# Subtracting the softmax maxima with 32-row products, maxima of the own chunk by query tile, and new durations for the planner

## The chip, the cores and the metric

One core of one Trainium2 chip runs the kernel. The metric is the device time of one execution in microseconds (us). The engines work side by side, each with its own list of instructions in a fixed order: PE (matrix products; its weight loads are listed apart as PEld), DVE (vector work), ACT (activations and copies), POOL (vector work away from the accumulators), SP (it issues the DMAs) and the DMA queues. Products accumulate in eight banks of 128 partitions by 512 fp32 words, which DVE and ACT read. Engines wait for each other by semaphores; while the first instruction of an engine's list waits, what is behind it waits too.

## The reference

Two transformer layers over 2048 tokens of width 256, each an attention and a gated FFN with layer norms around them. Layer 0 projects queries and keys through a small width with rotary parts, layer 1 through one matrix. What the change touches is the causal attention, which is the same in both layers: 16 heads of width 16.

```python
scores = jnp.einsum('bhqd,bhkd->bhqk', q_full, k_full) * scale
causal = jnp.tril(jnp.ones((T, T), dtype=bool))
scores = jnp.where(causal[None, None], scores, -jnp.inf)
probs = jax.nn.softmax(scores, axis=-1)
y = jnp.einsum('bhqk,bhkd->bhqd', probs, v)
...
x = x + _layernorm(_L0_attn_ref(_layernorm(x, axis=-1), ...), axis=-1)
x = x + _layernorm(_L0_ffn_ref(_layernorm(x, axis=-1), ...), axis=-1)
x = x + _layernorm(_L1_attn_ref(_layernorm(x, axis=-1), ...), axis=-1)
x = x + _layernorm(_L1_ffn_ref(_layernorm(x, axis=-1), ...), axis=-1)
```

## The kernel before

**Tiling.** The 2048 tokens are cut into four chunks `c` of 512 (`CH`), each of four tiles of 128 (`P`, `TPC = 4`). The 16 heads are four groups `g` of four; a group is two pairs `i` of two heads `e`. A unit is one chunk of queries with one group of heads: 16 units a layer, 32 in all, in the order (0,0), (0,1), all of chunks 1, 2 and 3, then (0,2), (0,3). Numbers are split into a high and a low half, so one head's scores contract over 64 rows (four products of halves of 16 values). Two heads of a pair thus lie on the two halves of the 128-row array: head `e` on rows 64e to 64e+63.

**One unit** has two parts.

The *maxima* (`maxima`) give each query's largest score. Queries are on the partitions. For every earlier chunk `p`, every query tile `t` and every head, one product of 64 rows by 512 keys fills a bank (L675) and DVE reduces it to one column of `pm` (L701, `pm<-banks 128x1<-128x512`). The own chunk is cut differently: `diagonal` writes the causal mask of all four diagonal tiles with a product of a 128x128 identity and `mask_qk` (L688, bf16, full array) and accumulates the four diagonal tiles of 128 keys onto it, the two heads by turns (L693); `block("b")` takes the keys left of the diagonal for query tiles 3 and 1 (384 and 128), `block("c")` those of tile 2 (256). DVE reduces each bank by 128-key tiles: the diagonals into column 1 of `pm`, the others into `pml`. `close` merges `pml` into column 0 of `pm` (three small reductions, also L701), takes the largest over all columns, and writes its negative as a high and a low half into `mx`. Four transposes (L737) and a copy on ACT (L741) turn it into `mrow`: rows 64e + 2i and 64e + 2i + 1 hold the two halves for head (i, e).

The *weighted sum* (`weighted`) goes over the 128-key tiles `kt`, up to the diagonal. Here keys are on the partitions. For each pair, a two-bank tile gets first the negative maxima, spread over all keys by a product with the selector `sel` that contracts over 64 rows, of which two hold something (L761, the shift), and then the scores on top (L766); both heads of the pair side by side, one on each half of the array. ACT takes the exponential into `pt` (L771). On a diagonal tile POOL zeroes what is masked (L775). Then the four heads' products with V (L782, 128 rows by 32 columns, four side by side, two instructions each) accumulate into one bank `av`, which is copied (L790), transposed (L795) and divided on DVE. On the last unit of a chunk follow the output projection, the norm and the sum with x (`mixed`).

**The order** of every instruction on every engine is written by a planner. Each piece of work is an `Op` with an engine, an estimated duration, the buffers that it reads and writes, a rank (lower is wanted earlier) and, on PE, a mode (`"row"`, `"col"` or `"full"`) and lanes (halves of the array). `Plan.run` simulates: of all ops that can start, it finds the earliest, and among ops of the same engine that could start up to `NEAR` later takes the lowest rank. `SWITCH` is what it allows for a change of mode, `HOP` for a semaphore, `lag` for an op's latency. Work comes out in exactly that order. Eight banks are shared; at most two two-bank tiles (`s`) are in use at a time. The maxima of a unit are ranked about one unit ahead of its weighted sum, so in a steady stretch PE mixes shifts, scores and V products of one unit with maxima of the next.

The FFN (`ffn`) has its own plan: for each chunk gate and up products (L912), SiLU and multiplication, splitting into halves (L923, L924), and the down product (L879). Projections and output products run through `products` (L553).

Of the kernel before, what the change touches and what calls it, by code (L numbers as in the profile page):

```python
# [132 lines left out]
class Plan:  # L133
# [3 lines left out]
    HOP, NEAR, SWITCH = 0.06, 0.3, 0.25  # L137

    def __init__(self):
        self.ops = []  # L140

    def op(self, engine, us, fn, r=(), w=(), after=(), hold=(), rank=0.0, mode=None, lanes=(0, 1), lag=0.0):
# [6 lines left out]
        o = Op(engine, us, fn, bufs, list(dict.fromkeys(deps)), rank, mode, lanes, lag)  # L149
# [9 lines left out]
    def run(self):  # L159
# [9 lines left out]
        while ready:  # L169
            best = []  # L170
            for o in ready:
# [26 lines left out]
                if o.engine == "PE":  # L198
                    at = max([at] + [free.get(("PE", x), 0.0) for x in o.lanes])
                    if o.mode != mode:  # L200
                        at = max([at] + [free.get(("PE", x), 0.0) for x in (0, 1)]) + self.SWITCH
                else:
                    at = max(at, free.get(o.engine, 0.0))
# [3 lines left out]
            at, o = min((p for p in best if p[1].engine == first[1].engine and p[0] <= first[0] + self.NEAR),  # L207
                        key=lambda p: (p[1].rank, p[0]))
# [27 lines left out]
def kernel(ctx: ExitStack, tc: tile.TileContext, x_in, cols_in, rows_in, wd_in, wuq_in, rot_in,  # L236
# [145 lines left out]
    ident16 = const.tile([P, P], BF16, tag="ident16", name="ident16")  # L382
    mask_qk = const.tile([P, TPC, P], BF16, tag="mask", name="mask")

    def make_mask():
        make_identity(nc, ident16)
        nc.gpsimd.memset(mask_qk, 0.0)
        nc.gpsimd.affine_select(out=mask_qk, in_=mask_qk, compare_op=ALU.is_ge, fill=NEG, base=0,
                                pattern=[[0, TPC], [-1, P]], channel_multiplier=1)

    mask_b = setup("POOL", 1.8, make_mask)


    sel_f = const.tile([P, 2, P], F32, tag="sel_f", name="sel_f")
    sel = const.tile([P, 2, P], F32R, tag="sel", name="sel")

    def make_sel():
        nc.gpsimd.memset(sel_f, 0.0)
        for e in range(2):
            for i in range(2):  # L400
                at = sel_f[64 * e:64 * e + 64, i, :]
                for row_ in (2 * i, 2 * i + 1):
                    nc.gpsimd.affine_select(out=at, in_=at, compare_op=ALU.not_equal, fill=1.0, base=-row_,
                                            pattern=[[0, P]], channel_multiplier=1)
        nc.gpsimd.tensor_copy(sel, sel_f)
# [4 lines left out]
    pms = [const.tile([P, TPC, 2, 2, NCHUNK + 1], F32, tag=f"pm{i}", name=f"pm{i}") for i in range(2)]  # L410

    def make_mx():
        for i in range(2):
            nc.gpsimd.memset(pms[i], NEG)
        for i in range(2):
            nc.gpsimd.memset(mx[i], 0.0)

    mx_b = setup("POOL", 1.6, make_mx)
# [27 lines left out]
    def normalize(plan, dst, src, rs, nm, i, r, w, rank):  # L446
        plan.op("ACT", 0.45, lambda: nc.scalar.activation(dst(), src(), AF.Identity, bias=nm.t[:, i:i + 1],
# [17 lines left out]
    def flipped(plan, src, hold, name, rank):  # L465

        banks = []
        for cc in range(2):
# [6 lines left out]
            plan.op("PE", 0.5, flip, r=[src], w=[s], hold=hold, rank=rank, mode="full", lag=0.2)  # L475
# [3 lines left out]
    def transposed(plan, src, name, rank):  # L479
        dst = wide_buf(f"T_{name}")  # L480
        for cc, s in enumerate(flipped(plan, src, [dst], name, rank)):
            plan.op("ACT", 0.59, lambda cc=cc, s=s: nc.scalar.copy(as_halves(dst.t)[:, cc, :], s.t), r=[s], w=[dst], rank=rank)
# [12 lines left out]
    def stacked(plan, c, what, s, i, bias, hi, lo, rank):  # L495

        plan.op("ACT", 0.69, lambda: nc.scalar.activation(as_halves(hi.t)[:, i, :], s.t, AF.Identity, bias=bias[:, i:i + 1]),
# [51 lines left out]
    def products(plan, s, us, terms, r, hold, rank):  # L549
# [5 lines left out]
        plan.op("PE", us, go, r=r, w=[s], hold=hold, rank=rank, mode="full", lag=0.2)  # L555

    def proj0(plan, c, rank, *dst):
# [23 lines left out]
        for i, (n, a, b) in ((1, (P, DQR, DC)), (0, (DQR, 0, DQR))):  # L581
# [6 lines left out]
            plan.op("PE", 0.5, flip, r=[cd, normed[i]], w=[s], hold=[cT], rank=rank, mode="full", lag=0.2)  # L588
# [56 lines left out]
    def attention(layer, plan, wo, wob, bo, scale):  # L645
        L, KS, Vs, kb, vb = layer.L, layer.K, layer.V, layer.kb, layer.vb
        with tc.tile_pool(name=f"kv{L}", bufs=1) as kv, tc.tile_pool(name=f"at{L}", bufs=1) as at:
# [4 lines left out]
            for tag in ("Q", "y", "pml", "mrow", "pt", "o"):  # L652
                rings.pop(tag, None)
            rpm, rmx = Ring(2), Ring(2)

            def maxima(n, c, g, qb):

                pm, mx_ = Buf(lambda: pms[n % 2], rpm), Buf(lambda: mx[n % 2], rmx)
                pml = new(at, [P, 2, 2, 6], F32, "pml", f"pml{L}{n}", 2)
                full = 2 * (2 * TPC * c + 6)  # L660
# [6 lines left out]
                def block(name, i, e, terms, us, reduces, red_us, kc, dst):  # L667

                    s = bank(f"m{L}{n}{i}{name}{e}")
                    b = 64 * e  # L670
                    rk = rank()

                    def fill():
                        for t, k0, k1, to in terms:
                            nc.tensor.matmul(s.t[:, to:to + k1 - k0], qb.t[b:b + 64, i, t * P:(t + 1) * P],  # L675
                                             KS[kc][b:b + 64, 2 * g + i, k0:k1], start=True, stop=True)

                    plan.op("PE", us, fill, r=[qb, kb[kc][g]], w=[s], hold=[dst], rank=rk, mode="row", lanes=(e,), lag=0.2)
                    plan.op("DVE", red_us, lambda: reduces(s.t), r=[s], w=[dst], rank=rk)

                def diagonal(i):

                    ss = [bank(f"m{L}{n}{i}d{e}") for e in range(2)]
                    rk = rank()

                    def fill():
                        for e in range(2):
                            nc.tensor.matmul(ss[e].t, ident16, mask_qk.rearrange("p t k -> p (t k)"), start=True, stop=False)  # L688
                        for t in range(TPC):
                            for e in range(2):  # L690
                                b = 64 * e
                                at_ = slice(t * P, (t + 1) * P)
# [405 lines left out]
```

## Time and profile before

| | |
|---|---|
| median of 3 runs | 1487.26 us (1486.95 to 1487.43) |
| the profiled execution | 1490.08 us |
| span of its instructions | 1488.4 us |
| mean granted clock of PE | 0.935 |
| shift products (L761) | 1280 instructions, 296.3 us busy |
| score products (L766) | 1280 instructions, 257.8 us busy |
| V products (L782) | 2560 instructions, 303.5 us busy |
| products for the maxima (L675, L693, L688) | 1152, 512 and 128 instructions; 261.8, 46.9 and 42.1 us busy |
| exponentials (L771, ACT) | 640 instructions, 548.1 us busy |
| reductions for the maxima (L701, DVE, large ones) | 1152 instructions, 687.5 us busy |

Busy times are sums of instruction records. On PE a record includes the time that a product waits in the array's pipe, and products on different halves overlap, so a record is longer than the pace at which products follow each other; the pace is read from starts. A group's line names the line of the code, the engine, the operation, its output and inputs with shapes, how often it runs, its busy time and mean, and the idle time of its engine before it with what ended it. `64*128 64x512` reads: 64 rows by 128 columns of the array, 512 columns streamed.

### The profile page before, as it was taken

The numbers are of one execution on the slowest core, as the hardware profiler recorded it, in microseconds if no ns is written. First come the engines' busy times: TensorE is split into PE (matmuls) and PEld (weight loads), VectorE is DVE, ScalarE is ACT, GpSimd is POOL, SyncE is SP. The second block draws the span as 40 slices with busy tenths as digits, with TensorE's granted clock in tenths as the row PEclk, the third lists the DMA queues.
The fourth block names the chain that finished last, engine by engine and source line by source line (L and its number), as shares of the span: only waits on it lengthen the run. The fifth ranks groups of instructions, "written<-read, shape, count | busy, mean of one in ns | idle before, by whom it ended". The sixth has DMA issues, their size and how long they took to land.

```text
span 1488.4 us, 22354 instructions
## 1 busy us (share of the span) xinstructions
PE 1325.1 (89%) x8632; PEld 740.4 (50%) x8632; DVE 934.5 (63%) x1932; ACT 798.0 (54%) x1094; POOL 289.6 (19%) x468
## 2 busy tenths in 40 slices
PE   2578999999999999959996999999999999995996
PEld 1344544544454444437764555455444444443875
DVE  1267679678888772424444756886888787333442
ACT  1232664556556668545551345555655666764563
POOL 3010111110001000235631101110000100023564
PEclk9687999899999999969997799999999999997998
DMA  4432230032000000020045023005000000000000
GB/s 148 173 134 90 73 141 28 2 125 75 15 15 1 15 15 16 1 71 0 1 170 212 15 91 122 15 15 183 17 15 15 1 15 15 15 1 1 1 29 29
DMA packets 42618, 78.74 MB, mean 53 GB/s; under 512 B 3891, under 2 KB 8336, under 8 KB 42384
## 3 DMA queue, kind: packets, MB, share of 16 engines
q1 hardware_dynamic: 42080, 75.85, 14.6%
q8 instruction: 67, 1.10, 0.3%
q0 software_dynamic: 144, 1.16, 0.2%
q10 hardware_dynamic: 288, 0.31, 0.1%
q14 instruction: 39, 0.32, 0.1%
HBM read 41.66 MB, written 35.65 MB: 52 GB/s over the span
## 4 chain that ended last, share of the span: by engine, by line
PE 64%; DVE 18%; ACT 6%; DMA 4%; POOL 3%; issue 3%; SPq 1%; POOLq 0%; ACTq 0%; DVEq 0%
PE banks L782 13%; PE banks L761 11%; DVE pm L701 11%; PE banks L675 9%; PE banks L766 8%; PE banks L553 8%; PE banks L912 5%; ACT pt L771 3%; PE banks L693 2%; DVE pml L701 2%; PE banks L688 2%; PE banks L879 2%; DMA Q<-sc_q 2%; PE banks L473 2%; PE banks L795 1%
## 5 line engine op out<-in xcount | busy, mean ns | idle before, releaser
L771 ACT ACTIVATE pt<-banks 128x1024 f32<-128x1024 f32 (+3 forms) x640 | 548.1, 895 | 362.2 <-PE banks L766 332.6
L701 DVE TENSOR_REDUCE pm<-banks 128x1 f32<-128x512 f32 (+1 forms) x896 | 557.8, 682 | 144.0 <-PE banks L675 73.4
L782 PE MATMUL banks<-pt,V 128*32 128x512 f32 (+3 forms) x2560 | 303.5, 545 | 6.7 <-POOL pt L775 6.4
L761 PE MATMUL banks<-mrow,sel 64*128 64x512 f32 (+3 forms) x1280 | 296.3, 429 | 14.6 <-DVE pm L701 5.2
L675 PE MATMUL banks<-K,Q 64*128 64x512 f32 (+3 forms) x1152 | 261.8, 414 | 16.7 <-ACT pt L771 3.5
L775 POOL TENSOR_SCALAR_AFFINE_SELECT pt<-pt 128x256 f32<-128x256 f32 x256 | 104.4, 411 | 870.2 <-ACT pt L771 868.0
L766 PE MATMUL banks<-Q,K 64*128 64x512 f32 (+3 forms) x1280 | 257.8, 373 | 0.0
L761 PEld LDWEIGHTS banks<-mrow,sel 64*128 64x128 f32 x1280 | 139.7, 191 | 197.1 <-ACT pt L771 99.2
L675 PEld LDWEIGHTS banks<-K,Q 64*128 64x128 f32 x1152 | 138.3, 192 | 142.7 <-DVE pm L701 62.1
L701 DVE TENSOR_REDUCE pml<-banks 128x4 f32<-128x512 f32 (+1 forms) x256 | 129.7, 549 | 95.1 <-PE banks L675 94.7
L766 PEld LDWEIGHTS banks<-Q,K 64*128 64x128 f32 x1280 | 143.6, 193 | 7.1
L782 PEld LDWEIGHTS banks<-pt,V 128*32 128x32 f32 x2560 | 52.4, 109 | 101.9 <-issue 76.0
L924 POOL TENSOR_TENSOR fl<-fu,fh 128x512 fp32r<-128x512 f32 x64 | 81.9, 1292 | 79.5 <-ACT fh L923 79.5
L921 DVE SCALAR_TENSOR_TENSOR fu<-banks,cols,sl 128x512 f32<-128x512 f32 x64 | 46.9, 747 | 58.1 <-ACT sl L919 42.0
L693 PE MATMUL banks<-K,Q 64*128 64x128 f32 x512 | 46.9, 307 | 32.1 <-DMA Q<-sc_q 32.1
L912 PE MATMUL banks<-fx,wg 128*128 128x512 f32 x256 | 73.9, 409 | 1.7 <-ACT sl L919 0.9
L912 PE MATMUL banks<-fx,wu 128*128 128x512 f32 x256 | 70.0, 396 | 0.0
L693 PEld LDWEIGHTS banks<-K,Q 64*128 64x128 f32 x512 | 37.5, 207 | 62.6 <-issue 49.8
L923 ACT CAST fh<-fu 128x512 fp32r<-128x512 f32 x64 | 39.5, 620 | 38.4 <-DVE fu L921 38.2
L912 PEld LDWEIGHTS banks<-fx,wg 128*128 128x128 f32 x256 | 48.7, 194 | 14.4 <-DVE fx L866 2.1
L912 PEld LDWEIGHTS banks<-fx,wu 128*128 128x128 f32 x256 | 49.4, 193 | 10.5
L919 ACT ACTIVATE sl<-banks,cols 128x512 f32<-128x512 f32 x64 | 43.1, 687 | 15.2 <-PE banks L912 14.9
(127 smaller groups left out, 1104.5 us busy)
## 6 DMA issues: line engine op xcount, KB each, us to landing
K<-sc_k SPq DMA_DIRECT2D x32, 512.0 KB
Q<-sc_q SPq DMA_DIRECT2D x32, 512.0 KB
sc_k<-kh SPq DMA_DIRECT2D x32, 256.0 KB
sc_k<-kl SPq DMA_DIRECT2D x32, 256.0 KB
sc_q<-qh SPq DMA_DIRECT2D x32, 256.0 KB
sc_q<-ql SPq DMA_DIRECT2D x32, 256.0 KB
x<-in_x_dram SPq DMA_DIRECT2D x4, 512.0 KB
out_dram<-x SPq DMA_DIRECT2D x4, 512.0 KB
```

What stands on the lines that cost most here:

```text
L553: nc.tensor.matmul(s.t[:, at:at + n], a, b, start=start, stop=stop)
L675: nc.tensor.matmul(s.t[:, to:to + k1 - k0], qb.t[b:b + 64, i, t * P:(t + 1) * P], KS[kc][b:b + 64, 2 * g + i, k0:k1], start=True, stop=True)
L693: nc.tensor.matmul(ss[e].t[:, at_], qb.t[b:b + 64, i, at_], KS[c][b:b + 64, 2 * g + i, at_], start=False, stop=t == TPC - 1)
L701: nc.vector.tensor_reduce(dst, src, AX.X, ALU.max)
L761: nc.tensor.matmul(s.t[:, e, 0:nq], sel[b:b + 64, i, :], mrow.t[b:b + 64, off:CH], start=True, stop=False)
L766: nc.tensor.matmul(s.t[:, e, 0:nq], KS[kt // TPC][b:b + 64, 2 * g + i, k * P:(k + 1) * P], qb.t[b:b + 64, i, off:CH], start=False, stop=True)
L771: plan.op("ACT", 0.19 + nq / 620, lambda s=s, pt=pt, nq=nq: nc.scalar.activation(pt.t[:, :, 0:nq], s.t[:, :, 0:nq], AF.Exp, scale=scale), ...
L775: plan.op("POOL", 0.41, lambda pt=pt: nc.gpsimd.affine_select(out=pt.t[:, :, 0:P], in_=pt.t[:, :, 0:P], compare_op=ALU.is_ge, fill=0.0, ba ...
L782: nc.tensor.matmul(av.t[32 * j:32 * j + 32, off:CH], Vs[kt // TPC][:, kt % TPC, DV * h:DV * h + 32], pts[kt, j // 2].t[:, j % 2, 0:nq], st ...
L912: nc.tensor.matmul(s.t[:, i, :], w[:, cc, fc * P:(fc + 1) * P], xT[j].t[:, cc, :], start=n == 0, stop=n == 3)
L921: plan.op("DVE", 0.75, lambda s=s, sl=sl, fu=fu, fc=fc: nc.vector.scalar_tensor_tensor(fu.t, s.t[:, 1, :], col(su_at + fc), sl.t, ALU.mult ...
L924: plan.op("POOL", 1.3, lambda fu=fu, fh=fh, fl=fl: nc.gpsimd.tensor_tensor(fl.t, fu.t, fh.t.bitcast(F32), ALU.subtract), r=[fu, fh], w=[fl ...
```

## The change

**Shifts.** The maxima's layout changes: head `h = 2i + e` of a group has its own 32 rows of `mrow` (rows 32h and 32h + 1 hold the two halves), and `sel` is one 128x128 tile with two rows of ones in each 32. A shift contracts over 32 rows; the two heads of pair `i` take rows 64i to 64i + 63, one half of the array. In the plan the shift becomes an op of its own with `lanes=(i,)`, ahead of the score op, which keeps both halves. Both have the mode `"row"`.

**Own-chunk maxima.** `diagonal` and `pml` go. Three blocks per head, `a` (query tile 3, 512 keys), `b` (tile 2 with 384 and tile 0 with 128) and `c` (tile 1 with 256), each write the mask for their diagonal tiles with two 64-row products (`half16` holds an identity cut in two halves of 64 rows), add the diagonal products, and then write the rest of the tile's keys. Each reduction covers one query tile's keys and writes column 0 of `pm`. All own-chunk blocks of a unit come first, then the other chunks.

**The planner.** New allowances for switching by the mode switched to, 0.11 us for a weight load, a latency for every op of DVE, ACT and PE; ops within 0.12 us of the earliest are considered instead of 0.3, and starting later is charged 0.3 of rank a microsecond (both 0.1 in the FFN's plan). ACT's estimated durations are some 0.09 us shorter.

```diff
-    HOP, NEAR, SWITCH = 0.06, 0.3, 0.25
-
-    def __init__(self):
-        self.ops = []
+    HOP, LOAD, SWITCH = 0.06, 0.11, {"row": 0.14, "col": 0.21, "full": 0.18}
+    LAG = {"DVE": 0.08, "ACT": 0.1, "PE": 0.2}
+
+    def __init__(self, near=0.12, waiting=0.3):
+        self.ops, self.near, self.waiting = [], near, waiting
...
                 if o.engine == "PE":
-                    at = max([at] + [free.get(("PE", x), 0.0) for x in o.lanes])
-                    if o.mode != mode:
-                        at = max([at] + [free.get(("PE", x), 0.0) for x in (0, 1)]) + self.SWITCH
+                    lanes, more = (o.lanes, 0.0) if o.mode == mode else ((0, 1), self.SWITCH[o.mode])
+                    at = max([at + self.LOAD] + [free.get(("PE", x), 0.0) + more for x in lanes])
...
-            at, o = min((p for p in best if p[1].engine == first[1].engine and p[0] <= first[0] + self.NEAR),
-                        key=lambda p: (p[1].rank, p[0]))
+            at, o = min((p for p in best if p[1].engine == first[1].engine and p[0] <= first[0] + self.near),
+                        key=lambda p: (p[1].rank + self.waiting * (p[0] - first[0]), p[0]))
...
-    ident16 = const.tile([P, P], BF16, tag="ident16", name="ident16")
-    mask_qk = const.tile([P, TPC, P], BF16, tag="mask", name="mask")
+    half16 = const.tile([P, 2, P], BF16, tag="half16", name="half16")
+    mask_qk = const.tile([P, 2, 2, P], BF16, tag="mask", name="mask")
...
-                def diagonal(i):
...
-                        for e in range(2):
-                            nc.tensor.matmul(ss[e].t, ident16, mask_qk.rearrange("p t k -> p (t k)"), start=True, stop=False)
-                        for t in range(TPC):
-                            for e in range(2):
-                                b = 64 * e
-                                at_ = slice(t * P, (t + 1) * P)
-                                nc.tensor.matmul(ss[e].t[:, at_], qb.t[b:b + 64, i, at_], KS[c][b:b + 64, 2 * g + i, at_],
-                                                 start=False, stop=t == TPC - 1)
...
+                        def part(t, k0, to, width, start, stop):
+                            nc.tensor.matmul(s.t[:, to:to + width], qb.t[b, i, t * P:(t + 1) * P],
+                                             KS[kc][b, 2 * g + i, k0:k0 + width], start=start, stop=stop)
+
+                        if kc < c:
+                            for t, k0, k1, to in terms:
+                                part(t, k0, to, k1 - k0, True, True)
+                            return
+
+                        lo = terms[0][3] + terms[0][2] - terms[0][1] - P
+                        for x in range(2):
+                            nc.tensor.matmul(s.t[:, lo:lo + P * len(terms)].rearrange("p (d k) -> p d k", k=P), half16[b, x, :],
+                                             mask_qk[b, x, 0:len(terms), :], start=x == 0, stop=False)
+                        for j, (t, k0, k1, to) in enumerate(reversed(terms)):
+                            part(t, k1 - P, to + k1 - k0 - P, P, False, j == len(terms) - 1)
+                        part(t, k0, to, k1 - k0 - P, True, True)
...
+                    for e in range(2):
+                        block("a", i, e, [(3, 0, CH, 0)], 0.45, c, [(0.6, 3, 0, slice(0, CH))])
+                    for e in range(2):
+                        block("b", i, e, [(2, 0, 3 * P, 0), (0, 0, P, 3 * P)], 0.8, c,
+                              [(0.47, 2, 0, slice(0, 3 * P)), (0.2, 0, 0, slice(3 * P, CH))])
+                    for e in range(2):
+                        block("c", i, e, [(1, 0, 2 * P, 0)], 0.4, c, [(0.34, 1, 0, slice(0, 2 * P))])
...
-                    for t, a, b in ((1, 3, 4), (2, 4, 6), (3, 0, 3)):
-                        top(pm.t[:, t, :, :, 0], pml.t[:, :, :, a:b])
...
+                        def shift(s=s, i=i, off=off, nq=nq):
+                            for e in range(2):
+                                b = slice(64 * i + 32 * e, 64 * i + 32 * e + 32)
+                                nc.tensor.matmul(s.t[:, e, 0:nq], sel[b], mrow.t[b, off:CH], start=True, stop=False)
+
+
+                        plan.op("PE", max(0.19, nq / 2220), shift, r=[mrow, sel_b], w=[s], rank=rk, mode="row", lanes=(i,))
+
                         def score(s=s, kt=kt, i=i, off=off, nq=nq):
-                            for e in range(2):
-                                b = 64 * e
-                                nc.tensor.matmul(s.t[:, e, 0:nq], sel[b:b + 64, i, :], mrow.t[b:b + 64, off:CH],
-                                                 start=True, stop=False)
...
-                        plan.op("PE", 2 * max(0.19, nq / 2380), score, r=[qb, mrow, kb[kt // TPC][g], sel_b], w=[s], rank=rk,
-                                mode="row", lag=0.2)
-                        plan.op("ACT", 0.19 + nq / 620, lambda s=s, pt=pt, nq=nq: nc.scalar.activation(
+                        plan.op("PE", max(0.19, nq / 2220), score, r=[qb, kb[kt // TPC][g], s], w=[s], rank=rk,
+                                mode="row")
+                        plan.op("ACT", 0.1 + nq / 620, lambda s=s, pt=pt, nq=nq: nc.scalar.activation(
...
-            plan = Plan()
+            plan = Plan(0.1, 0.1)
```

In the changed kernel the same work has other line numbers: shifts L753, scores L762, maxima L679, masks L689, V products L778.

## The prediction

> **What bounds the kernel now.** I read the page first: busy shares, then the chain of work that ended last.
>
> ```profile
> PE 1325.1 (89%) x8632; PEld 740.4 (50%) x8632; DVE 934.5 (63%) x1932; ACT 798.0 (54%) x1094; POOL 289.6 (19%) x468
> PE 64%; DVE 18%; ACT 6%; DMA 4%; POOL 3%; issue 3%; SPq 1%; POOLq 0%; ACTq 0%; DVEq 0%
> ```
>
> PE carries the end, DVE is second. A share over the whole span mixes stages, so next come busy times in four stretches: attention of layer 0, FFN, attention of layer 1, FFN (columns: stretch, length, each engine's busy time and instructions, granted clock, DMA share, GB/s).
>
> ```profile
> 95.00:655.00 560.00, 525.59 (x3754) 268.92 (x3752) 394.63 (x805) 320.32 (x412) 74.07 (x160) 0.95 0.14 50
> 655.00:800.00 145.00, 126.54 (x530) 95.30 (x530) 65.95 (x145) 76.78 (x134) 65.37 (x60) 0.94 0.21 73
> 800.00:1345.00 545.00, 515.92 (x3680) 260.68 (x3682) 385.13 (x760) 309.06 (x388) 64.58 (x135) 0.95 0.13 45
> ```
>
> Attention is 1105 of 1488 us; what the change touches lies there. DMA moves little, ACT has a third free. Then the chain by line in a steady part of it (950 to 1250 us, clock 1.00):
>
> ```profile
> by line: PE banks L782 17.9%; DVE pm L701 17.1%; PE banks L761 16.1%; PE banks L675 14.4%; PE banks L766 10.2%; ACT pt L771 5.6%; PE banks L553 4.7%; issue 3.9%; PE banks L693 2.2%; PE banks L688 1.9%; DVE pml L701 1.8%; PE banks L795 1.2%;
> ```
>
> The PE lines add up to 69%, DVE to 19%. So of a microsecond of PE work added or removed I count 0.69 on the path. A busy PE record includes waiting in its pipe, so prices come from starts. PE in order of time:
>
> ```profile
> 1171.25 0.62 PE L675 MATMUL banks<-K,Q 64*128 64x512 f32 x4
> 1171.81 1.07 PE L782 MATMUL banks<-pt,V 128*32 128x512 f32 x8
> ...
> 1173.14 0.41 PE L766 MATMUL banks<-Q,K 64*128 64x512 f32 x2
> 1173.37 0.41 PE L761 MATMUL banks<-mrow,sel 64*128 64x512 f32 x2
> 1173.60 0.41 PE L766 MATMUL banks<-Q,K 64*128 64x512 f32 x2
> ...
> 1177.98 0.60 PE L688 MATMUL banks<-mask,ident 128*128 128x512 bf16 x2
> 1178.51 0.66 PE L693 MATMUL banks<-K,Q 64*128 64x128 f32 x8
> 1179.01 0.45 PE L761 MATMUL banks<-mrow,sel 64*128 64x512 f32 x2
> ```
>
> Two 64-row products on the two halves of the array, 512 columns each, start a new pair every 0.23 us (1173.14, 1173.37, 1173.60), weights included. Four L675 before L782 take 0.56, that is 2 x 0.23 and 0.10 more: the array changes from 64 rows by 128 columns to 128 rows by 32. Two L688 before L693 take 0.53, 0.07 more: there the row height alone changes, 128 to 64. So a change of array form costs 0.07 to 0.10; I use 0.09. The eight L693 (four pairs of 128 columns) take 0.50, 0.125 a pair, against 128/512 x 0.23 = 0.055 of streaming: with short products the weight load sets the pace, 0.07 over the stream.
>
> **The change, part by part.** What follows counts along the order in which each kernel issues to PE.
>
> *Shifts.* There are 320 key tiles, of mean width 435 columns (139264 columns in all), 0.85 of 512. Before, each has two shift pairs, each filling both halves: 640 x 0.85 x 0.23 = 125 us. After, a pair fills one half, and two pairs can run side by side. Only 101 key tiles have all four shifts next to each other; the other 219 have them as 438 separate pairs with 64-row products, V products or transposes between. If a 32-row product doesn't share the array with 64-row ones, this is (101 + 438) x 0.85 x 0.23 = 105: **-20 us**. If it does, at best 320 x 0.85 x 0.23 = 63: -62.
>
> *Changes of form.* If 32 rows and 64 rows are two forms, the order has 1488 changes after against 851 before (729 of the new ones between 32 and 64 rows): 637 x 0.09 = **+57 us**. If they are one form, 759: -92 x 0.09 = -8. No 32-row product is in this trace. The lower bound of a 32-64 change is 0 (L766 to L761 goes from one half's products to the next without a gap), the upper is 0.10 of L675 to L782; the nearest row is L688 to L693, row height alone, and it pays. So I take 0.09, and the other end is the first rival.
>
> The Trainium skill, TensorEngine Tiling (Array Packing), section Key Properties, says that changing the tiling mode, and not just the tile, drains the array, and its Available Configurations list 32x128 apart from 64x128. That agrees with the 0.07 to 0.10 and speaks against this change; without that rule the sum would be the rival's. TensorE: Matmul & The Clock Gate, Measured speedup vs the span model, gives 3.07 times for four 32-row products side by side, not 4; by it the 101 full runs would take 0.30 instead of 0.23 each, an estimate of 6 us more. No run here shows either for 32 rows.
>
> *Maxima over other chunks* (768 products of 512 columns). Their work is the same, but shifts now stand between the two halves' products: a run of them takes the fuller half, and these add up to 459 slots before, 558 after: 99 x 0.23 = **+23 us**. With one form the neighbour fills the half: 0.
>
> *Own-chunk maxima.* Per pair of heads, before: two 512-column masks, four 128-column pairs alternating between the halves, then 384, 128 on each half and 256 on each. PE starts in order, so a half's product runs beside the other's last one only: 1024 + 512 + 1152 = 2688 columns. After, each half gets its whole block (4, 5 or 4 products) before the other: counted the same way 3200 columns. 512 more columns are 0.23 us, x 64 pairs: +15. Loads: ten of the 26 products are 128-column f32r ones, 0.07 over stream each, against 4 x 0.07 before: 0.42 x 64 = +27. Bounds: 0 if the loads hide, +63 if the eight 128-column mask products pay too; I take the middle one, because the mask's weights are bf16 and their load record is half as long (L688 101 ns on average, L693 207). Together **+42 us**.
>
> Sum on PE: -20 + 57 + 23 + 42 = +102, x 0.69 = **+70 us**.
>
> *DVE.*
>
> ```profile
> L701 DVE TENSOR_REDUCE pm<-banks 128x1 f32<-128x512 f32 x768 | 476.8, 681 | 74.6 <-PE banks L675 73.4 <-PE banks L766 0.2
> L701 DVE TENSOR_REDUCE pml<-banks 128x4 f32<-128x512 f32 x128 | 82.5, 682 | 51.0 <-PE banks L675 50.8
> L701 DVE TENSOR_REDUCE pml<-banks 128x2 f32<-128x256 f32 x128 | 49.7, 416 | 44.2 <-PE banks L675 43.9
> L701 DVE TENSOR_REDUCE pm<-pml x96: 143/152/164, 88.1 to 1339.3; 128x4 f32<-128x4 f32 x32, 128x4 f32<-128x8 f32 x32, 128x4 f32<-128x12 f32 x32
> ```
>
> The 96 merges of pml go: -96 x 0.152 = -15 us. Per head the reduces were 512, 512, 256 wide (0.685 + 0.682 + 0.416 = 1.78 us) and become 512, 384, 128, 256: the 384 one lies between 0.416 and 0.681 (0.55), the 128 one between 0.152 and 0.416 (0.28), 1.93: +0.15 x 128 = +19. Net +4, x 0.19 = **+1**. The merges stood before the transpose of the maxima (L737), so that latency shortens by 0.45 us a unit, 32 units; PE has scores of the unit before to run there, so I count nothing (14 us if that cover were gone).
>
> *Nothing:* ACT keeps its 961 issues and SP its 171; the DMA order differs in five places, and DMA is 13% busy. The set-up on POOL (mask, selector, zeroing) is about the same few microseconds between 10 and 17 us, long before the first mask product at 58 us. The split of shift from score adds no semaphore wait: the wait for the bank pair (freed by the exponential, L771) and for mrow moves to the shift, the wait for Q and K to the score. What is queued behind either on PE is the next maxima or V product; DVE waits for the first, ACT for the second, which frees its output buffers.
>
> *The planner.* New durations, a narrower choice and a penalty for waiting change the order on all engines, FFN too. A better order can only take what PE waits for others: the shift's weight loads sat 104 us until the exponential and 62 until a maximum, 166 in all, but they are loads, and mostly hidden. I take a twentieth, **-8**, with bounds -40 (a quarter) and +20 (the new planner knows no 32-64 change, so its times are off by 0.09 at each of 729).
>
> Sum: 70 + 1 - 8 = +63. The profiled execution took 1490.1 (span 1488.4 and 1.7 around it), 2.8 over the median of the runs, 1487.3; the difference goes on the median: **1550 us**. With the bounds (changes at 0.07, loads 0, planner -40, and half of it on the path; or 0.10, 63, +20 and all on the path) this case runs from 1495 to 1610.
>
> **Rivals.** *32 and 64 rows share the array without a change (faster).* For: 64-row products of the two halves run side by side, and a shift sits in one half. Against: L688 to L693 pays for row height alone. Price on PE: between -62 + 42 - 8 = -28 and, counted along the order with both halves free (row-form products and masks take 406 us at 0.23 for 512 columns, before 434; loads +27, changes -8), -9; the middle -18 x 0.69 = -12, planner -8: **1467**, 1440 to 1490. It decides from a 32-64 change below about 0.01 us.
>
> *PE's waits swallow it.* DVE's 19% and ACT's 6% of the chain become the bound and PE's 102 us fall into its waiting. Against: PE lines are 69% of the chain. Then +1 - 8: 1480; with part of it, **1490**.
>
> *The weight load can't be fetched ahead over a 32-64 change.* Each would show a load record, 0.19 us (L761 PEld), instead of 0.09: 637 x 0.10 x 0.69 = 44 more, **1594**, up to 1640. For: loads are ahead only if their rows are free. Against: at L675 to L782 a load of 0.11 and a change fit in 0.10.
>
> **How the numbers follow.** Forecast 0.62; one form 0.28; swallowed 0.06; load exposed 0.04. About 0.2% (3 us) is what a measurement tells from no change. Faster: 0.25 of the second, 0.02 of the third and 0.01 of the first, 0.28; within 0.2%: 0.05; slower: 0.67. The range 1455 to 1605 leaves out about 0.07 below (the one-form case with a good plan) and 0.09 above. Both signs hold much of the chance; the likeliest case's own range is 1495 to 1610.
>
> **What would show it.** From the start of a shift pair (L753) to the following score (L762), without a wait between: 0.32 if it is a change of form, 0.23 if not. A 64-row product right behind a shift on the other half: starting with it, or 0.3 later. Own-chunk blocks: 2.1 us per pair of heads, or 1.4. PE's share of the chain should rise above 69% in the steady stretch. Wrong would be: shifts starting beside maxima of the other half; or PE no longer in the chain.

## The result, and the profile after

| | before | after |
|---|---|---|
| median of the runs taken together | 1487.11 us (1484.84 to 1487.43, 4 runs) | 1610.45 us (1593.79 to 1620.85, 4 runs) |
| ratio of the fast runs, 95% interval | 1 | 1.0796 (1.0703 to 1.0888) |
| the profiled execution, its span | 1490.08, 1488.4 | 1593.79, 1592.1 |
| mean granted clock of PE | 0.935 | 0.920 |

The change costs 8%. One run of after (1620.85 us) counts as slow, being over 1.5% above its quickest; the other three have a median of 1605.1 us (1593.79 to 1615.8), 118 us over before, and what follows goes by these. The profiled execution is the quickest of all, so its trace explains 104 us of the 118.

The page of after, busy shares and then the chain that ended last, by engine:

```profile
PE 1442.5 (91%) x9272; PEld 789.6 (50%) x9272; DVE 938.2 (59%) x1964; ACT 794.7 (50%) x1094; POOL 289.3 (18%) x468
PE 75%; DVE 8%; DMA 5%; ACT 4%; issue 3%; POOL 2%; SPq 2%; POOLq 0%; ACTq 0%; DVEq 0%
```

PE is 117 us busier, DVE and ACT within 4 us of what they were, and DVE's part of the chain went from 18% to 8%: PE has become the bound outright. By stage (stretch, length, each engine's busy time and instructions, granted clock, DMA share, GB/s; the same four stages as before, the last FFN left out):

```profile
95.00:700.00 605.00, 578.26 (x3989) 286.23 (x3987) 391.54 (x792) 318.25 (x410) 72.16 (x150) 0.93 0.13 46
700.00:850.00 150.00, 133.86 (x549) 99.83 (x550) 64.07 (x145) 77.24 (x135) 65.23 (x67) 0.92 0.21 71
850.00:1450.00 600.00, 575.52 (x4005) 285.59 (x4003) 390.15 (x788) 305.95 (x384) 62.92 (x136) 0.93 0.12 42
```

Attention went from 560 to 605 us in the first layer and from 545 to 600 in the second: 100 of the 104 us, with DVE's and ACT's work in it within some 5 us of what it was. The chain by line in a steady part of the second (1110 to 1240 us; clock 0.50 in its first 13 us, 1.00 behind):

```profile
by line: PE banks L778 25.4%; PE banks L679 22.4%; PE banks L753 19.3%; PE banks L762 12.6%; DVE pm L697 7.5%; PE banks L557 2.8%; PE banks L689 2.7%; ACT pt L767 2.7%; issue 1.7%; PE banks L791 1.5%; PE banks L729 1.4%; ACTq L767 0.0%; DVE
```

PE's lines add up to 88% (before: 69%). What PE holds up is the exponential. Its row in before and in after:

```profile
L771 ACT ACTIVATE pt<-banks 128x1024 f32<-128x1024 f32 (+3 forms) x640 | 548.1, 895 | 362.2 <-PE banks L766 332.6
L767 ACT ACTIVATE pt<-banks 128x1024 f32<-128x1024 f32 (+3 forms) x640 | 546.4, 895 | 491.2 <-PE banks L762 392.8
```

ACT works as long as before but sits idle before exponentials for 491 us in place of 362, 393 of them until a score. Now where PE's time goes. Products and weight loads of after in order of time, clock 1.00:

```profile
1191.18 0.50 PE L753 MATMUL banks<-mrow,sel 32*128 32x512 f32 x2
1191.61 0.18 PEld L679 LDWEIGHTS banks<-K,Q 64*128 64x128 f32 x1 [0.25 <-issue]
1191.61 0.49 PE L679 MATMUL banks<-K,Q 64*128 64x512 f32 x1
1192.03 0.19 PEld L753 LDWEIGHTS banks<-mrow,sel 32*128 32x128 f32 x2 [0.24 <-issue]
1192.03 0.50 PE L753 MATMUL banks<-mrow,sel 32*128 32x512 f32 x2
...
1192.46 0.49 PE L679 MATMUL banks<-K,Q 64*128 64x512 f32 x1
1192.47 0.95 PE L762 MATMUL banks<-Q,K 64*128 64x512 f32 x4
1192.81 0.41 PEld L679 LDWEIGHTS banks<-K,Q 64*128 64x128 f32 x2
...
1193.03 0.39 PE L679 MATMUL banks<-K,Q 64*128 64x512 f32 x1
```

Shift, maxima, shift, maxima follow each other at 0.43 us (1191.18, 1191.61, 1192.03, 1192.46), where 512 columns stream in 0.23. So each change between 32 and 64 rows costs 0.20. The loads show half of why: at a change the load starts with its product (1191.61, 1192.03), while inside the 64-row run the loads of L679 start at 1192.81 for a product at 1193.03, 0.22 ahead. The first weights after a change are loaded in the open. This holds throughout: in the traces of before, after and the first experiment, at clock 1.00, the load starts at most 4 ns ahead of its product at 95% or more of the changes between 64 rows, 32 rows and V products; within runs of the 64-row form it is ahead by 0.06 to 0.17 us in the median.

Was this to be seen before? Yes, in lines that the prediction's excerpt passed over. PE of before, again in order of time:

```profile
1170.69 0.50 PE L761 MATMUL banks<-mrow,sel 64*128 64x512 f32 x2
1171.02 0.39 PE L766 MATMUL banks<-Q,K 64*128 64x512 f32 x2
...
1172.80 0.50 PE L761 MATMUL banks<-mrow,sel 64*128 64x512 f32 x2
```

The shift at 1172.80 comes right behind V products, and the score behind it started at 1173.14: 0.34, against 0.23 for the pairs that followed (1173.14, 1173.37, 1173.60). The prediction measured a change by how late the *new* form starts (0.10 from L675 to L782) and didn't look at the pair after it, where the other 0.11 lies. My count over both traces, and over that of the first experiment below: pairs of 64-row products on both halves, 512 columns, clock 1.00; us from their start to the next start (median, and how many):

```
place in the run of one form    before         after          experiment 1
first after a change            0.337 (178)    0.337 (225)    0.338 (219)
between                         0.234 (634)    0.234 (191)    0.234 (532)
last before V or 32 rows        0.327 (130)    0.326 (66)     0.340 (57)
the only one                    none           0.431 (35)     0.433 (1)
```

The first pair of a run takes 0.10 more than one between and the last takes 0.09 more; a run of one pair takes both. This price was the same before; after has three times fewer pairs between.

### The profile page after: what moved, and what is told of

The parts are those of the page before. It is cut to its first block, busy times and chain, and to the rows that moved or that the text cites. A ratio compares the mean times of both kernels' runs of the same rounds, so it can differ in the third digit from the quotient of the medians.

```text
span 1592.1 us, 23654 instructions
## 1 busy us (share of the span) xinstructions
PE 1442.5 (91%) x9272; PEld 789.6 (50%) x9272; DVE 938.2 (59%) x1964; ACT 794.7 (50%) x1094; POOL 289.3 (18%) x468
## 4 chain that ended last, share of the span: by engine, by line
PE 75%; DVE 8%; DMA 5%; ACT 4%; issue 3%; POOL 2%; SPq 2%; POOLq 0%; ACTq 0%; DVEq 0%
PE banks L778 16%; PE banks L679 15%; PE banks L753 13%; PE banks L762 9%; PE banks L557 7%; PE banks L908 6%; DVE pm L697 4%; DMA Q<-sc_q 3%; PE banks L689 3%; PE banks L875 2%; ACT pt L767 2%; PE banks L477 2%; SPq L515 1%; PE banks L729 1%; PE banks L791 1%
## 5 line engine op out<-in xcount | busy, mean ns | idle before, releaser
L697 DVE TENSOR_REDUCE pm<-banks 128x1 f32<-128x512 f32 (+3 forms) x1280 | 697.0, 603 | 273.8 <-PE banks L679 255.0
L679 PE MATMUL banks<-K,Q 64*128 64x512 f32 (+3 forms) x1664 | 402.4, 407 | 43.8 <-DMA Q<-sc_q 41.7
L778 PE MATMUL banks<-pt,V 128*32 128x512 f32 (+3 forms) x2560 | 314.2, 561 | 2.7 <-POOL pt L771 1.8
L679 PEld LDWEIGHTS banks<-K,Q 64*128 64x128 f32 x1664 | 227.0, 209 | 132.4 <-issue 49.8
L762 PE MATMUL banks<-Q,K 64*128 64x512 f32 (+3 forms) x1280 | 281.0, 412 | 0.0
L753 PE MATMUL banks<-mrow,sel 32*128 32x512 f32 (+3 forms) x1280 | 263.9, 472 | 11.5 <-ACT pt L767 9.8
L753 PEld LDWEIGHTS banks<-mrow,sel 32*128 32x128 f32 x1280 | 107.0, 186 | 263.6 <-ACT pt L767 171.2
L762 PEld LDWEIGHTS banks<-Q,K 64*128 64x128 f32 x1280 | 143.6, 190 | 61.0 <-issue 53.2
L689 PE MATMUL banks<-mask,half 64*128 64x128 bf16 (+1 forms) x768 | 108.4, 265 | 9.5 <-DVE pm L697 4.3
L778 PEld LDWEIGHTS banks<-pt,V 128*32 128x32 f32 x2560 | 53.1, 110 | 87.8 <-issue 71.1
L689 PEld LDWEIGHTS <-half 64*128 64x128 bf16 x768 | 45.4, 101 | 51.4 <-issue 47.5
L798 DVE RECIPROCAL r<-banks 128x16 f32<-128x16 f32 x32 | 8.1, 252 | 101.8 <-PE banks L791 101.8
```

The source lines that it names most:

```text
L679: nc.tensor.matmul(s.t[:, to:to + width], qb.t[b, i, t * P:(t + 1) * P], KS[kc][b, 2 * g + i, k0:k0 + width], start=start, stop=stop)
L689: nc.tensor.matmul(s.t[:, lo:lo + P * len(terms)].rearrange("p (d k) -> p d k", k=P), half16[b, x, :], mask_qk[b, x, 0:len(terms), :], sta ...
L697: plan.op("DVE", red_us, lambda t=t, p=p, src=src: nc.vector.tensor_reduce(pm.t[:, t, i, e, p:p + 1], s.t[:, src], AX.X, ALU.max), r=[s], ...
L753: nc.tensor.matmul(s.t[:, e, 0:nq], sel[b], mrow.t[b, off:CH], start=True, stop=False)
L762: nc.tensor.matmul(s.t[:, e, 0:nq], KS[kt // TPC][b:b + 64, 2 * g + i, k * P:(k + 1) * P], qb.t[b:b + 64, i, off:CH], start=False, stop=True)
L778: nc.tensor.matmul(av.t[32 * j:32 * j + 32, off:CH], Vs[kt // TPC][:, kt % TPC, DV * h:DV * h + 32], pts[kt, j // 2].t[:, j % 2, 0:nq], st ...
```

## Experiments

Every comparison has three or more rounds against the kernel before; its median in these was 1485 to 1487 us. All of the kernels compute the full result.

**1. The order of after, shifts of 64 rows.** Each shift contracts over 64 rows again, head `e` on half `e`, with `sel` and the layout of the maxima as before; every engine issues the same work in the same order as in after.

```diff
-                                b = slice(64 * i + 32 * e, 64 * i + 32 * e + 32)
-                                nc.tensor.matmul(s.t[:, e, 0:nq], sel[b], mrow.t[b, off:CH], start=True, stop=False)
+                                b = 64 * e
+                                nc.tensor.matmul(s.t[:, e, 0:nq], sel[b:b + 64, i, :], mrow.t[b:b + 64, off:CH],
+                                                 start=True, stop=False)
```

> The changed kernel with its order of instructions kept on every engine; only the shift products contract over 64 rows again, head e on half e, as before the change. In the order the changes of array form fall from 1488 to 759; shift streams rise from 105 to 125 us. Theory 1 (a change of form costs 0.20 us: 0.10 for the change and 0.10 because the first product behind it loads its weights in the open): PE work falls by 729 x 0.20 - 20 = 126 us, of which 0.7 to 1 is on the path: 1485 to 1525 us. Theory 2 (32-row products are cheap; the loss comes from the own-chunk blocks and the new order): within 20 us of 1610. Forecast's price (0.09 a change): 1610 - 0.7 x (66 - 20) = about 1575.

Measured: 1507.3 us (1505.0 to 1509.1), ratio 1.0133 (1.0111 to 1.0156). With the order held, the form alone is worth 98 of the 118 us by the medians (85 by the two profiled executions, since that of after is its quickest). It takes the changes of form from 1515 to 786, 729 fewer. (Changes are counted here and below along the weight loads of each whole trace; before has 877. The expectations leave some stages out, with the same differences within some twenty.) The page of this kernel (busy shares, chain by engine, the exponentials):

```profile
PE 1340.3 (89%) x9272; PEld 793.2 (53%) x9272; DVE 930.8 (62%) x1964; ACT 791.0 (52%) x1094; POOL 289.8 (19%) x468
PE 69%; DVE 12%; DMA 7%; ACT 5%; issue 3%; POOL 2%; SPq 2%; POOLq 0%; ACTq 0%; DVEq 0%
L770 ACT ACTIVATE pt<-banks 128x1024 f32<-128x1024 f32 (+3 forms) x640 | 543.8, 896 | 408.8 <-PE banks L765 330.7
```

PE's busy time falls by 102 us with the same 9272 products, the idle time before exponentials by 82, and DVE's part of the chain is back at 12%. The last column of the count above is this kernel's: nearly three times as many starts between, and one lone run in place of 35.

The granted clock has a part in this. After ran 254 us of its profiled span at clock 0.50, this kernel 197 (before 194). As the order is the same, the two traces can be set side by side, in blocks of 20 products: where both have the full clock throughout, after is 66 us longer, and 645 of the 729 changes lie there; where only one of them has it, after is 19 us longer in sum; where neither has, they are equal. So over three quarters of the 85 us stand apart from the clock. Whether the changes of form also bring the lower clock, no run separates.

**2. The shifts of 32 rows alone.** Before, with the new layout of maxima and the shift split from the score; the planner and the own-chunk maxima are the old ones.

```diff
-                        def score(s=s, kt=kt, i=i, off=off, nq=nq):
+                        def shift(s=s, i=i, off=off, nq=nq):
...
-                                b = 64 * e
+                                b = slice(64 * i + 32 * e, 64 * i + 32 * e + 32)
```

> The kernel before with the 32-row shifts alone (own-chunk maxima and planner as before; the planner orders them itself). Changes of form rise by about 660. Theory 1: 660 x 0.20 = 132, less 20 of shift streams, x 0.7 to 1: 1565 to 1600 us. Theory 2: 1470 to 1495 us.

Measured: 1608.5 us (1607.2 to 1615.8), ratio 1.0829 (1.0799 to 1.0860), slightly above what was expected. This part alone brings all of the loss, under another order. Changes of form go from 877 to 1530: 122 us over 653 is 0.19 us of time for each, but this includes what the split and the clock do: 297 us of its span ran at clock 0.50, against 194 in before.

**3. After without the 32-row shifts.** Shift and score are one op of the plan again, 64 rows; the new planner and own-chunk maxima stay, and the plan comes out anew. The edit is the reverse of the second's.

> The changed kernel with the shifts as before (64 rows, both halves, one op with the scores), the planner ordering anew: own-chunk maxima and planner of the change alone. About 40 changes of form fewer than in the same-order run. Theory 1: 1475 to 1515 us. Theory 2: 1580 or more.

Measured: 1561.6 us (1558.5 to 1565.2), ratio 1.0505 (1.0477 to 1.0533): 47 us over the range expected, with only 741 changes of form. Something else costs here, and the next run says what.

**4. The planner alone.** Before, with the new durations, switches, latencies and choice.

```diff
-    HOP, NEAR, SWITCH = 0.06, 0.3, 0.25
+    HOP, LOAD, SWITCH = 0.06, 0.11, {"row": 0.14, "col": 0.21, "full": 0.18}
+    LAG = {"DVE": 0.08, "ACT": 0.1, "PE": 0.2}
...
+    def __init__(self, near=0.12, waiting=0.3):
```

> The kernel before with the new planner and durations alone. Changes of form 718 against 763 (transposes not counted): 45 x 0.20 = 9 us less on PE. Theory 1 and the forecast: 1465 to 1490 us. Theory 2 (the order costs): 1520 or more.

Measured: 1552.8 us (1551.3 to 1555.6), ratio 1.0447 (1.0425 to 1.0469), where a little gain or nothing was expected. With 852 changes of form, fewer than before, this is no matter of forms. Busy times in three stretches of it (stretch, length, PE, PEld, DVE, ACT, POOL, clock, DMA share, GB/s):

```profile
380.00:400.00 20.00, 19.85 (x148) 9.82 (x149) 16.49 (x36) 12.60 (x14) 0.41 (x1) 1.00 0.01 2
410.00:440.00 30.00, 29.48 (x115) 15.86 (x114) 22.83 (x44) 6.43 (x10) 2.34 (x6) 0.53 0.05 18
440.00:460.00 20.00, 19.97 (x157) 9.84 (x149) 8.22 (x15) 16.02 (x19) 0.81 (x2) 1.00 0.00 1
```

In the steady mix DVE and ACT are both kept busy (first line). Here the order puts maxima together and then scores together: from 410 to 440 us ACT is busy 6 of 30 us, PE issues 115 products against 148 in 20 us, and the granted clock is 0.53; afterwards DVE is busy 8 of 20. Mean clock over the run: 0.899. It ran 313 us at clock 0.50 (the third experiment 313 too), against 194 in before. If PE set the pace in all of that time, the lower clock would account for 59 of the 61 us by which the span is longer; this estimate, half of the difference in time at 0.50, is an upper bound, for in part of it DVE sets the pace.

**5. The 32-row form made known to the planner.**

```diff
-    HOP, LOAD, SWITCH = 0.06, 0.11, {"row": 0.14, "col": 0.21, "full": 0.18}
+    HOP, LOAD, SWITCH = 0.06, 0.11, {"row": 0.14, "col": 0.21, "full": 0.18, "row32": 0.2}
...
-rank=rk, mode="row", lanes=(i,))
+rank=rk, mode="row32", lanes=(i,))
```

> The changed kernel, with one thing told to the planner: the 32-row shifts are a form of their own, and a change to it costs 0.2 us. Nothing else. Changes of form (transposes left out of the count) fall from 1401 to 1288. If a change costs 0.2 us and four fifths of it reach the path (as in the same-order run: 103 us gained for 729 changes less 20 us of streams): 113 x 0.2 x 0.8 = 18 less: 1585 to 1600 us. If changes don't set the time: 1610, within its spread of 1594 to 1621, or worse by the new order.

Measured: 1781.2 us (1779.7 to 1783.0), ratio 1.1977 (1.1952 to 1.2002), a wide miss: 1391 changes of form are left, and the mean clock falls to 0.857. Told the price, this planner, which chooses one op at a time, doesn't find an order with few changes. 507 us of its span of 1778 ran at clock 0.50, against 254 in after; why its order runs so was not followed further.

**6. Own-chunk maxima with halves by turns.** The first experiment, with the own-chunk blocks of a pair's two heads as one op, product by product on alternate halves.

```diff
+                        def part(t, k0, to, width, start, stop):
+                            for e in range(2):
+                                b = slice(64 * e, 64 * e + 64)
+                                nc.tensor.matmul(ss[e].t[:, to:to + width], qb.t[b, i, t * P:(t + 1) * P],
+                                                 KS[c][b, 2 * g + i, k0:k0 + width], start=start, stop=stop)
```

> The same-order 64-row kernel (1507 us) with the own-chunk blocks of the two heads of a pair issued as one op, the halves by turns product by product. My term for own-chunk maxima (+42 us on PE because a half's whole block goes before the other's) predicts PE 0.6 us less per pair of heads: 64 x 0.6 x 0.7 = 27 us less, 1475 to 1490 us. If these blocks hide behind DVE (their reductions take 3.9 us per pair of heads, more than the products): within 6 us of 1507.

Measured: 1529.6 us (1527.9 to 1534.7), ratio 1.0291 (1.0263 to 1.0318). It became slower than the first experiment, not faster. As one op it also came out in another order, so it tells nothing of the term by itself.

**7. The own-chunk maxima alone.** Before, with the blocks `a`, `b` and `c` of the change in place of `diagonal` and `pml`.

> The kernel before with the own-chunk maxima of the change alone (old planner, 64-row shifts). On PE +42 us for the blocks, 125 changes of form fewer (638 against 763, transposes left out) at 0.2 = -25: +17 x 0.7 = +12: 1490 to 1508 us. If the blocks hide and the changes count: 1487 - 18 = 1465 to 1480 us.

Measured: 1491.0 us (1488.8 to 1492.3, 10 runs), ratio 1.0029 (1.0018 to 1.0040), 4 us, at the lower edge of what was expected. This order has 783 changes of form against 877.

**8. The split without the form.** The fourth, with the 64-row shift as an op of its own that the plan puts on one half.

```diff
-                        def score(s=s, kt=kt, i=i, off=off, nq=nq):
+                        def shift(s=s, i=i, off=off, nq=nq):
...
+                        plan.op("PE", max(0.19, nq / 2220), shift, r=[mrow, sel_b], w=[s], rank=rk, mode="row", lanes=(i,))
```

> The new planner with the own-chunk maxima as before and 64-row shifts, but the shift an op of its own ahead of the scores and planned on one half, as in the change (the planner alone, with shift and scores as one op, gave 1553). If the new planner loses because with the one op it ranks maxima behind the weighted sums, so that stretches with DVE alone follow (in its trace ACT is idle and the granted clock 0.5 from 410 to 440 us): 1475 to 1500 us. If the new planner's choice loses whatever the ops: 1540 or more, and the own-chunk maxima of the change would be worth 40 us.

Measured: 1523.5 us (1520.9 to 1527.6), ratio 1.0238 (1.0213 to 1.0263), between the two expectations: under the new planner the split wins back 29 of the 66 us of the fourth. It doesn't do so by fewer changes of form, of which this order has 907.

**9 and 10. The planner's choice.** After, and the fourth, each with the old choice among ops (0.3 us, no charge for waiting) and the new durations.

```diff
-    def __init__(self, near=0.12, waiting=0.3):
+    def __init__(self, near=0.3, waiting=0.0):
```

> The changed kernel, with only the planner's choice as before (ops within 0.3 us of the earliest, the lowest rank first, nothing charged for waiting); new durations and allowances stay. Changes of form (transposes left out) 1353 against 1401. If the new choice costs something beside the 32-row products: 1560 to 1595 us (the 20 us that the same-order 64-row kernel is over before, and 48 x 0.2 x 0.8 = 8). If it doesn't: 1600 to 1620.

> The kernel before with the new durations and allowances but the old choice among ops (the planner whole gave 1553). If the choice is what separates maxima from weighted sums: 1480 to 1500 us. If the durations do it: 1530 or more.

Measured: after with the old choice 1626.0 us (1614.8 to 1632.7), ratio 1.0930 (1.0878 to 1.0982), above both expectations; before with the durations alone 1504.2 us (1502.9 to 1506.2), ratio 1.0122 (1.0098 to 1.0146), 4 us above the first. So of the fourth's 66 us the durations are 18 and the choice 48; but in the changed kernel the new choice costs nothing that these runs show (their spreads touch).

**11 and 12. Fewer changes from before.** V products of two key tiles as one op, in before and in the seventh.

```diff
+                    if kt % 2 == 0:
+                        continue
...
+                        for k in (kt - 1, kt):
+                            off = max(0, k - TPC * c) * P
+                            for j in range(4):
```

> The kernel before, the V products of two key tiles issued as one op, so that the array changes to the 128x32 form half as often: 458 changes of form against 763 (transposes left out). At 0.2 us a change, four fifths of it on the path: 305 x 0.2 x 0.8 = 49 us less: 1435 to 1465 us, the upper end if the six output buffers of the exponential (three key tiles) now hold up ACT. If a change costs 0.09 us or hides: 1465 to 1490.

> The same with the own-chunk maxima of the change (old planner, 64-row shifts): 339 changes of form against 638 in the kernel with these maxima alone (1491 us): 299 x 0.2 x 0.8 = 48 us less: 1440 to 1470 us. If changes hide: about 1490.

Measured: 1522.7 us (1522.1 to 1524.7), ratio 1.0245 (1.0226 to 1.0265), and 1514.2 us (1511.7 to 1518.0), ratio 1.0188 (1.0163 to 1.0212). The changes of form fell from 877 to 585 and from 783 to 490, and both kernels became slower than those they started from, by 36 and 23 us, where 49 and 48 us less were expected. ACT's waits in the first of the two (what waited and for what: us in total, times, longest):

```profile
ACT pt L771 <- PE banks L766: 282.7, 253, 5.2
ACT pt L771 <- PE banks L787: 82.1, 42, 6.1
```

The wait for scores fell from 332.6 us in before to 282.7, but a new one of 82.1 has come: exponentials wait for V products (L787) to free the `pt` buffers, 42 times. The two together are 32 us longer than before's one. In the second they are 248.9 and 112.8, against 372.7 and nothing in the seventh, so 11 us shorter, and yet it is 23 us slower. That the buffers take back what fewer changes give is thus a reading that fits the first alone; more buffers were not tried, no version beat the kernel before, and what a change to or from V products costs on the path is not shown.

## Why the prediction was wrong in size

It was right in direction, and right that 32 and 64 rows are two forms. The time lies 60 us above the forecast and just outside its range by the median of all four runs, 55 us above and at the range's end by that of the three. By its steps:

- *Changes of form, 637 x 0.09 = +57.* **This is the step that failed.** The count was right and the price was half. A change costs 0.20 us by the starts. By the first experiment it is 102 us of PE's busy time and the 20 us of streams that the 64-row shifts need more (125 against 105 in the prediction), over 729: 0.17; busy time at half clock is in that figure, while the 0.20 is from starts at full clock. It is the price of the last rival, which named the mechanism (the load isn't fetched ahead) and got 0.04. Its counter-argument, "at L675 to L782 a load of 0.11 and a change fit in 0.10", held the new form's first start to be the whole price; the start of a product says nothing of when it can stream. With 0.20 the term is +127 and the prediction's own sum gives (-20 + 127 + 23 + 42) x 0.69 + 1 - 8 = 112, about 1599; the three runs have 1594 to 1616. That it comes so near is in part luck: the own-chunk term looks too high and the share of 0.69 too low, and the sum has no term for the clock, where 19 of the first experiment's 85 us lie.
- *The test that it set itself:* 0.32 from a shift to the next score if a change of form, 0.23 if not. Measured 0.43 for a run of one shift pair: neither. The excess over 0.32 comes with a load that isn't fetched ahead. A 64-row product behind a shift on the other half was to start with it or 0.3 later: it starts 0.43 later.
- *Shifts, -20.* My reading of all starts at full clock in after: a run of one pair takes 0.256, 0.313, 0.368 and 0.427 us to the next form at 128, 256, 384 and 512 columns, the same 0.445 ns a column as before and 0.20 fixed; a run of all four shifts takes 0.435 at 512 columns. So the streams behave as costed. The Trainium skill, TensorE: Matmul & The Clock Gate, section Measured speedup vs the span model, gives a speedup of 3.07 for four 32-row products side by side; here four cost 0.008 more than two, and the measurement decides. The Trainium skill, TensorEngine Tiling (Array Packing), section Key Properties, says that changing the tiling mode drains the array; this fits the 0.09 at the end of a run of one form, though no run here shows that it is a drain.
- *Own-chunk maxima, +42 on PE, 29 on the time.* Too high, it seems. One pair's block in after, where no wait falls inside:

```profile
1200.16 0.30 PE L689 MATMUL banks<-mask,half 64*128 64x128 bf16 x4
...
1201.33 0.44 PE L762 MATMUL banks<-Q,K 64*128 64x512 f32 x1
...
1201.55 0.45 PE L762 MATMUL banks<-Q,K 64*128 64x512 f32 x1
...
1202.23 0.27 PE L689 MATMUL banks<-mask,half 64*128 64x128 bf16 x2
```

  From the first mask to the next pair's first mask it is 2.07, with one pair of scores inside; less 0.23 that is 1.84, between the forecast 2.1 and 1.4. Put into before alone, the part costs 4 us, and that with 94 fewer changes of form, which may hide part of it. The term by itself stays open.
- *Planner -8, unpaired maxima +23 on PE (16 on the time).* Together the forecast was +8 on the time; the first experiment less the seventh is +16. But before and the experiments 1, 3, 4, 6, 7, 8 and 10, the orders that have 64-row shifts and no joined V products, lie between 1487 and 1562 us with 741 to 907 changes of form, and the one with the fewest is the slowest: an order's cost is not the sum of such terms. The clock, which the prediction left out, differs between them: 313 us at 0.50 in the slowest, 194 in before. The bound of +20 for the planner held in the changed kernel and would not have held alone (+66).
- *PE's share of the chain, 0.69 for each microsecond.* It rose to 88% in the steady stretch, as forecast in direction. Between after and the first experiment 102 us of PE's busy time went with 85 us of the span: 0.83, both with the clock's part in them.
- *DVE, +4 busy.* Measured 938.2 - 934.5 = 3.7. *Nothing* for ACT, SP and the set-up: ACT's busy time fell by 3 us.
- *Rivals.* One form: refuted by the 0.43 and by the first experiment. Swallowed by PE's waits: the reverse, DVE fell from 18% to 8% of the chain.
- *Its bounds.* The likeliest case's range, 1495 to 1610, doesn't come out of the bounds that are named for it: all of them together give about 1480 at the low end and at least 1638 at the high end, and the measured time lies between these. ACT was idle for over two fifths of attention (57% busy), not a third; nothing rested on it.

The account that the runs support: 98 us the form, the clock's part included (after less the first experiment; 85 to 111 by the extremes of their runs), 16 the order (first less seventh), 4 the own-chunk part (seventh less before). The first is one edit with the order held; the other two hold only for these orders.

## What to carry to other kernels

Price a change of array form from starts on both sides of it: how late the new form starts, and how much longer its first product takes than the second. Count the changes in the order issued, and weigh a smaller row height against them: here 32 rows saved 20 us of streams and added 729 changes at 0.20. A planner that chooses greedily must be tried together with each edit, since its order alone moved the kernel before by 4% (the fourth experiment) and the changed one by 11% (the fifth). Compare the time at half clock before reading a difference between two orders as work.

## What was not expected of the hardware

- A change between 32 and 64 rows costs 0.20 us in either direction, whether the next 64-row product is on the shift's half of the array or on the other (0.43 each, at 512 columns; 63 and 60 cases, the half told by the order of issue). Starts give 0.09 at the end of a run and 0.10 at the beginning of the next; that the one is the emptying of the array and the other the open load is my reading, and no run separates them.
- The granted clock fell to a half without PE pausing long. The third experiment, where maxima stand alone in the order (columns as above):

```profile
1245.00:1260.00 15.00, 15.00 (x45) 8.70 (x46) 15.00 (x26) 0.00 (x0) 0.00 (x0) 0.50 0.00 0
1260.00:1280.00 20.00, 20.00 (x60) 11.87 (x59) 19.93 (x42) 0.59 (x1) 0.00 (x0) 0.50 0.00 0
1300.00:1320.00 20.00, 20.00 (x154) 8.04 (x150) 0.00 (x0) 18.79 (x20) 0.00 (x0) 1.00 0.00 1
```

  For 35 us PE issues three products a microsecond, as fast as DVE frees their banks, its records say 100% busy, and the clock is 0.50 throughout; with shifts and scores at 7.7 a microsecond it is 1.00. What makes the clock fall was not tried.
